# A fused transformer block on one core: expert biases gathered per slot, experts' rows found by a table of token ids, and three first-pass products in seven

## The chip, the cores and the metric

The kernel runs on one core of one Trainium2 chip. The metric is the device time in microseconds (us). The core has a matrix engine (PE in the profile, with its weight loads as PEld), a vector engine (DVE), a scalar engine (ACT), GpSimd (POOL), and SyncE (SP), which here issues the plain transfers; indirect transfers are issued by POOL. Matmul results go to PSUM, operands lie in SBUF, large arrays in DRAM.

## The reference

Two layers work on 8 x 256 = 2048 tokens of 512 channels, all in float32. What the change concerns is the first layer:

```python
xn = layernorm(x)
# attention with decay, 32 heads of 128 channels
q, k, v = silu(xn @ qkv_w.T)
out = gate * normed(attention(q, k, v)) @ out_w.T          # gate = sigmoid(xn @ gate_w.T)
# experts: each token goes to 2 of 16
y = sum over chosen e of ge[e] * (h_e @ w3[e] + b3[e])      # h_e = silu(xn @ w1 + b1) * (xn @ w2 + b2)
z = (silu(xn @ sw1 + sb1) * (xn @ sw2 + sb2)) @ sw3 + sb3   # shared expert
x = x + out + y + z
```

The second layer is a softmax attention with one head of 128 channels and a low-rank mixture of 64 parts; the change touches it in one place, where the last quarter of the residual is fetched.

## The kernel before, in words

**Chunks and the opening (L140 to L525).** The tokens are four chunks of 512 (NCH), each four tiles of 128 rows. In the opening, for each chunk, `normalize` and `turn_rows` give the transposed tokens xT, `token_sums` the sums that the fast products need, `shared_up` and `shared_down` the shared expert, `route` the two chosen experts of each token (`sel_all`) and their gates (`ge`). `shared_down` starts with the experts' last biases: the gates, with a column of ones for the shared bias, are turned by PE (L333), copied by ScalarE (L335) and multiplied by the 17 x 512 matrix of biases (L338) in front of the shared expert's own matmuls (L340). `clear(i)` writes zeros over a DRAM array `xd` of 47 x 128 slots. Behind the chunks, L447 to L523 work out for each token and choice its slot in a list sorted by expert (`slots`), its gate there, and for each tile of 128 slots its expert's weight rows (`rows_`).

**Four passes (L599 to L1215).** Each chunk is one pass i, of 8 groups g of four heads. A group is seven outer products p1 to p7 (a 2 x 2 split of the projection in Strassen's form with seven products instead of eight), in the order of `ORDER`. Each outer product is itself a 2 x 2 product. In passes 1 to 3 its inner products are seven too (`p1()` to `p3()`, L1037 to L1066): some banks are copied by ScalarE (`copied`), joined by DVE and added by POOL (`result`). In the first pass it has eight plain ones (`plain`, L981). The first pass reads the weights from their input array; for the outer products p1, p2 and p4 (`RAW`) they are used as they lie there, for the others DVE first forms outer sums of two or three blocks. POOL then forms four inner sums (`inner_sum`, L634), which are stored in DRAM (`ws`) for the three later passes. An inner product (`product`, L661) is four matmuls of 128 x 128 x 128. Three weight buffers go round (`big`), two staging buffers (`staged`).

**Order.** PE, DVE and SP are ordered by the framework's planner; ScalarE and POOL keep the written order inside the passes (`manual_schedule`, L599), but each engine executes its own list in order. Other work is put between the inner products by `later(after, f)` and `slot()`: every inner product is a slot, and a piece becomes due `after` slots later. So scores, attention, output products, and the experts are interleaved with the projections. `prepare(n + 2)` starts the load of the outer product two ahead; the sums of the next one's weights are made a step per slot (`following.step()`).

**Experts.** In the first pass two tiles of tokens per group are loaded (`row`, L1086) and scattered by POOL to their two slots of `xd` (`scatter`, L1093). From the second pass on, each of 47 tiles of slots is an `Expert` (L689), two or three per group: a plain load of its 128 rows from `xd` (L696), an indirect load of its expert's weights (L697), the turn on PE (L706) 8 slots later, the up product at 11 (L716), the down product at 14 (L728), which ScalarE copies (L733) and SP stores to `yd`. In the last layer the rows are gathered from `yd`, multiplied by the gates and added (`gather`, `settle`).

**End of a pass.** `load_sum` (L933) fetches the stored residual (`xr`, with shared expert and biases), `finish` adds the pass's output. For the last chunk this is done in the last layer (`next_x`, L1289).

## Time and profile before

| | |
|---|---|
| device time, three runs | 2856.99 us median (2852.0 to 2861.1) |
| profiled execution, its own time | 2856.16 us |
| its span, first to last instruction | 2854.4 us |
| mean granted PE clock | 0.993 |
| opening, 0 to 164 us | PE busy 143.8, DVE 96.3, POOL 81.9 us; clock 0.94 |
| first pass, 164 to 765 us | PE busy 588.1, DVE 373.4, POOL 353.3 us; DMA share 0.90 |
| three passes, 765 to 2532 us | PE busy 1752.5 of 1767 us, DVE 909.9, POOL 962.0 us |
| last layer, 2532 us to the end | PE busy 312.2 of 322.4 us |

Busy time is the union of an engine's instructions; matmuls are pipelined, so that a busy PE is occupied but not always at its peak. An "idle before" entry names what released an engine from a wait. DMA share is the mean busy share of the core's 16 DMA engines. Line numbers in the profile are those of the kernel's file; L97 is the helper through which all additions and subtractions go, so those are told apart by their tiles.

### The profile page before, as it was taken

The page shows a single profiled execution, that of the slowest core. Times are in us where ns is not written, and L with a number is a line of the kernel's source. Part 1 is how long each engine was busy: PE and PEld are TensorE (multiplying, and loading weights), DVE is VectorE, ACT ScalarE, POOL GpSimd, SP SyncE. Part 2 cuts the span into 40 slices and gives each one's busy share as a digit, 9 for nine tenths or more (in the row PEclk, how much of TensorE's full clock was granted, in tenths as well). Part 3 has the DMA queues.
Part 4 walks back from the last instruction along what each step waited for, and adds up shares of the span by engine and source line. Part 5 has one row for each costly group of instructions (what it writes and reads, how often), then busy time and mean ns, then how long its engine had stood idle before and what let it go on. Part 6 is the DMA issues. An engine that isn't in the chain of part 4 may idle for free. (4 is left out here: it accounts for less than half of the span.)

```text
span 2854.4 us, 49572 instructions
## 1 busy us (share of the span) xinstructions
PE 2796.7 (98%) x19864; PEld 2566.1 (90%) x19864; DVE 1569.7 (55%) x2615; ACT 948.2 (33%) x1683; POOL 1465.7 (51%) x1213
## 2 busy tenths in 40 slices
PE   8989999999999999999999999999999999999999
PEld 4469999999999999999999999999999999987877
DVE  6555666666654445444545555555555555556663
ACT  3312222212244333333443333443444333432221
POOL 4545666665546555555645454545544566552210
PEclk9999999999999999999999999999999999999999
DMA  7888998899986777778877777777777788652211
GB/s 255 301 309 337 357 352 341 341 349 347 364 320 246 262 266 273 282 270 299 296 265 257 264 266 265 259 274 280 284 259 259 267 310 298 222 212 88 76 61 61
DMA packets 161943, 763.21 MB, mean 267 GB/s; under 512 B 18209, under 2 KB 24225, under 8 KB 109874
## 3 DMA queue, kind: packets, MB, share of 16 engines
q1 hardware_dynamic: 149826, 706.25, 66.9%
q0 software_dynamic: 11888, 53.79, 5.2%
q8 instruction: 157, 2.57, 0.4%
q14 instruction: 72, 0.59, 0.1%
HBM read 596.14 MB, written 163.05 MB: 266 GB/s over the span
## 5 line engine op out<-in xcount | busy, mean ns | idle before, releaser
L666 PE MATMUL ps_a<-xt,w 128*128 128x128 f32 x5376 | 750.9, 276 | 11.7 <-DVE r L97 7.7
L666 PEld LDWEIGHTS ps_a<-xt,w 128*128 128x128 f32 x5376 | 681.9, 192 | 30.1 <-issue 14.3
L97 POOL TENSOR_TENSOR c<-c 128x512 f32<-128x512 f32 x216 | 271.7, 1273 | 262.0 <-DVE c L97 259.9
L97 POOL TENSOR_TENSOR c<-c,r 128x512 f32<-128x512 f32 x240 | 318.4, 1347 | 158.9 <-DVE r L97 153.1
L666 PE MATMUL ps_e<-xt,w 128*128 128x128 f32 x2688 | 373.4, 275 | 1.3 <-DVE c L97 1.3
L97 POOL TENSOR_TENSOR sums<-sums,sq 128x512 f32<-128x512 f32 x120 | 153.3, 1278 | 426.4 <-ACT sq L796 425.6
L996 ACT COPY cp<-ps_a 128x512 f32<-128x512 f32 x336 | 196.4, 585 | 476.0 <-PE ps_a L666 468.8
L666 PEld LDWEIGHTS ps_e<-xt,w 128*128 128x128 f32 x2688 | 344.4, 192 | 11.2 <-issue 3.8
L97 POOL TENSOR_TENSOR w<-w 128x512 f32<-128x512 f32 x224 | 294.6, 1325 | 108.2 <-issue 31.2
L666 PE MATMUL ps_a<-w,xt 128*128 128x128 f32 x1792 | 346.7, 275 | 0.0
L858 PE MATMUL ps_sc<-wo,gT 128*128 128x256 f32 x1288 | 305.1, 379 | 1.8 <-POOL gT L97 1.8
L97 DVE TENSOR_TENSOR acc<-ps_sc,acc 128x512 f32<-128x512 f32 x208 | 143.3, 690 | 265.8 <-PE ps_sc L858 198.8
L666 PEld LDWEIGHTS ps_a<-w,xt 128*128 128x128 f32 x1792 | 272.3, 192 | 0.0
L97 DVE TENSOR_TENSOR c<-ps_a,c 128x512 f32<-128x512 f32 x232 | 157.9, 686 | 202.7 <-PE ps_a L666 201.7
L858 PEld LDWEIGHTS ps_sc<-wo,gT 128*128 128x128 f32 x1288 | 232.3, 190 | 26.8 <-POOL gT L97 2.0
L666 PE MATMUL ps_b<-xt,w 128*128 128x128 f32 x1680 | 236.4, 277 | 6.8 <-ACT c L1010 4.2
L801 DVE SCALAR_TENSOR_TENSOR gT<-ps_o,nw,c 128x256 f32<-128x256 f32 x256 | 112.0, 479 | 231.0 <-ACT sq L796 222.0
L666 PEld LDWEIGHTS ps_b<-xt,w 128*128 128x128 f32 x1680 | 217.3, 194 | 17.5 <-issue 8.2
L744 ACT ACTIVATE c<-c 128x512 f32<-128x512 f32 x256 | 148.9, 627 | 170.1 <-DVE c L97 170.0
L796 ACT ACTIVATE sq<-ps_o 128x512 f32<-128x512 f32 x120 | 71.6, 597 | 382.3 <-PE ps_o L782 382.3
L666 PE MATMUL ps_e<-w,xt 128*128 128x128 f32 x896 | 173.2, 275 | 0.0
L97 DVE TENSOR_TENSOR s<-ps_sc,decay 128x384 f32<-128x384 f32 x256 | 139.8, 552 | 40.7 <-PE ps_sc L770 38.1
(299 smaller groups left out, 4635.8 us busy)
## 6 DMA issues: line engine op xcount, KB each, us to landing
w<-in_w_att_dram SPq DMA_DIRECT2D x128, 1024.0 KB
st<-in_w_att_dram SPq DMA_DIRECT2D x32, 1024.0 KB
wo<-in_w_out_dram SPq DMA_DIRECT2D x113, 256.0 KB
decay<-dec SPq DMA_DIRECT2D x64, 384.0 KB
w<-ws0p SPq DMA_DIRECT2D x12, 1792.0 KB
w<-ws1p SPq DMA_DIRECT2D x12, 1792.0 KB
w<-ws2p SPq DMA_DIRECT2D x12, 1792.0 KB
w<-ws3p SPq DMA_DIRECT2D x12, 1792.0 KB
```

The lines of the kernel that those rows point to most:

```text
L97: (eng or nc.vector).tensor_tensor(o, a, b, op)
L666: mm(bank[:, bass.ts(ty, P)], a, b, start=(first and ty == 0), stop=True, skip_group_check=True,)
L744: nc.scalar.activation(qk, qk, AF.Silu)
L796: nc.scalar.activation(sq, po, AF.Square)
L801: nc.vector.scalar_tensor_tensor(gT[:, h, :].rearrange("p (t n) -> p t n", t=2), po[:, bass.ts(h, S)].rearrange("p (t n) -> p t n", t=2), ...
L858: mm(py[:, bass.ts(t, S)], self.O[p][:, hh, bass.ts(t, P)], self.wo[p][:, hh, :], start=(t == 0 and hh == 0), stop=(hh == 1), skip_group_c ...
L996: nc.scalar.copy(c, bank)
```

## The change

*Last biases.* The gates' column of ones, the turn of the gates, their copy and the bias matmuls leave the opening. Each expert tile gathers its expert's bias row into all 128 partitions (an indirect transfer of POOL, `bias`, by the new list `own_`) into the space that its tokens had, and DVE adds it as it takes the down product out of PSUM, where ScalarE had copied it. The shared expert's bias is added by POOL to the residual where it is fetched (`last_bias`).

*Rows by a table.* `xd`, its clearing, the loads of rows and their scatters go. The 32 scatters stay, five per group, but write only token ids into a DRAM table of one integer per slot. In the first pass's last group the table is read and turned (`read_table`, one PE transpose), and each expert's tokens are gathered from the stored normalized tokens by an indirect transfer of POOL. The turn, bias, up and down stand at 10, 12, 13 and 18 slots.

*Sevenfold.* In the first pass, the outer products p1, p2 and p4 are made of seven inner ones as in the later passes, with the tokens' sums formed once by POOL (`first_sums`). Their inner weight sums come in a new order, that of 7 first, and those that are left when the outer product starts are made ahead of it. The next weights are prepared behind the last product of the outer product before.

*Space.* `before`, `sel_all` and the gates move from the opening's pool to the space of the accumulator; `dist` moves into the opening's pool. The store of the residual keeps its written place.

```diff
-    def once(shape, name):
-        return work.tile(shape, FP, tag=name, name=name, bufs=1)
+    def once(shape, name, dtype=FP):
+        return work.tile(shape, dtype, tag=name, name=name, bufs=1)
+    disp = Parts(accp.tile([P, 7 * CH], FP, tag="acc", name="disp"))
...
-    b3_t = held[0 : E + 1, SH * C : (SH + 1) * C]
-    nc.sync.dma_start(out=b3_t, in_=b3)
...
-    xd = dram.tile([NSLOT, C], FP, name="xd")
+    table = dram.tile([NSLOT, 1], I32, name="table")
...
-    xnd = [dram.tile([P, TPC, C], FP, name=f"xnd{i}") for i in range(NCH)]
+    xnd = dram.tile([NT, C], FP, name="xnd")
...
-    zero = held[:, (SH + 1) * C : (SH + 2) * C].unsqueeze(1)
-    nc.gpsimd.memset(zero, 0.0)
+    none = once([NMT, P], "none", I32)
+    nc.gpsimd.memset(none, 0)
+    nc.sync.dma_start(out=table.rearrange("(j p) o -> j (p o)", p=P), in_=none)
...
-        tt(ge[:, :, 0:E], sc, sel, ALU.mult)
-        nc.vector.memset(ge[:, :, E : E + 1], 1.0)
+        tt(ge, sc, sel, ALU.mult)
...
         xc = xs[i]
-        pg = ps_sc()
-        for t in range(TPC):
-            nc.tensor.transpose(pg[0 : E + 1, bass.ts(t, P)], gates[i][:, t, :], ident)
-        gT = work.tile([E + 1, CH], FP, tag="geT", name="geT", bufs=1)
-        nc.scalar.copy(gT, pg[0 : E + 1, :])
...
-            mm(py, gT[:, bass.ts(t, P)], b3_t, start=True, stop=False)
...
-                mm(py, hT[:, e, bass.ts(t, P)], w3sh[:, e, :], start=False, stop=(e == SH - 1))
+                mm(py, hT[:, e, bass.ts(t, P)], w3sh[:, e, :], start=(e == 0), stop=(e == SH - 1))
...
-    sel_all = once([P, NTT, E], "sel_all")
+    sel_all = disp.tile([P, NTT, E], FP, name="sel_all")
...
-        nc.sync.dma_start(out=xr[i], in_=xs[i])
+        tc.keep_in_program_order(nc.sync.dma_start(out=xr[i], in_=xs[i]))
...
             if i == 0:
+                t = first_x[p]
...
-                    nc.sync.dma_start(out=blocks(first_x[p][:, 0:4]), in_=y)
+                    nc.sync.dma_start(out=blocks(t[:, 0:4]), in_=y)
+                if p in RAW:
+                    first_sums.append(t)
...
-    def clear(i):
-        lo, hi = (0, 12, 24, 36, NMT)[i : i + 2]
-        nc.sync.dma_start(
-            out=xd[lo * P : hi * P, :].rearrange("(j p) c -> p j c", p=P),
-            in_=zero.to_broadcast([P, hi - lo, C]),
-        )
...
-        nc.sync.dma_start(out=xnd[i], in_=xns[i])
+        nc.sync.dma_start(
+            out=xnd[i * CH : (i + 1) * CH, :].rearrange("(t p) c -> p t c", p=P), in_=xns[i]
+        )
...
-        ge = once([P, TPC, E + 1], f"ge{i}")
+        ge = disp.tile([P, TPC, E], FP, name=f"ge{i}")
...
-        clear(i)
...
-    disp = Parts(accp.tile([P, 7 * CH], FP, tag="acc", name="disp"))
+    own_ = const.tile([P, NMT], I32, name="own_")
+    whose = const.tile([P, NMT], I32, name="whose")
+    token = const.tile([P, NTT], I32, name="token")
+    nc.gpsimd.iota(token, pattern=[[P, NTT]], base=0, channel_multiplier=1)
...
+    def last_bias(r, t3):
+        nc.sync.dma_start(out=t3, in_=b3[E : E + 1].to_broadcast([P, C]))
+        for t in range(TPC):
+            add(r[:, t, :], r[:, t, :], t3, nc.gpsimd)
...
                     f(w[:, o], w[:, a_], w[:, b_], pool)
-                    if o == 7:
+                    if o == 6:
...
-                    partial(inner_sum, *at) for at in ((add, 4, 0, 3), (sub, 5, 4, 1), (sub, 6, 2, 5), (sub, 7, 1, 0))
+                    partial(inner_sum, *at) for at in ((sub, 7, 1, 0), (add, 4, 0, 3), (sub, 5, 4, 1), (sub, 6, 2, 5))
...
+                if p in RAW:
+                    return sums_of(w)
...
+            return sums_of(w)
+        def sums_of(w):
...
+            if i == 0 and p in RAW:
+                x_ = first_x[p]
+                return dict(zip(("p1", "p7", "p2", "p3", "p5", "p6", "p4"), (x_[:, n] for n in range(7))))
...
                 )
+        for t in first_sums:
+            sub(t[:, 4], t[:, 1], t[:, 0], nc.gpsimd)
+            sub(t[:, 1], t[:, 3], t[:, 1], nc.gpsimd)
+            sub(t[:, 5], t[:, 3], t[:, 4], nc.gpsimd)
+            sub(t[:, 6], t[:, 2], t[:, 5], nc.gpsimd)
...
-                n += getattr(f, "func", f).__name__ not in ("silu", "gate", "row", "scatter", "load_sum", "sums1", "sums2", "sums3", "sums4", "settle0", "settle1", "out_sum")
+                n += getattr(f, "func", f).__name__ not in ("silu", "bias", "gate", "read_table", "scatter", "load_sum", "sums1", "sums2", "sums3", "sums4", "settle0", "settle1", "out_sum")
...
                 self.xe, self.we = xw[:, 0:C], xw[:, C:]
-                nc.sync.dma_start(out=self.xe, in_=xd[bass.ts(j, P), :])
+                nc.gpsimd.indirect_dma_start(
+                    out=self.xe, out_offset=None, in_=xnd[:, :],
+                    in_offset=bass.IndirectOffsetOnAxis(ap=whose[:, j : j + 1], axis=0),
+                    bounds_check=NT - 1, oob_is_err=False,
+                )
...
+
+            def bias(self):
+                nc.gpsimd.indirect_dma_start(
+                    out=self.xe, out_offset=None, in_=b3[:, :],
+                    in_offset=bass.IndirectOffsetOnAxis(ap=own_[:, self.j : self.j + 1], axis=0),
+                    bounds_check=E, oob_is_err=False,
+                )
...
                 ye = attn.tile([P, C], FP, tag="sum", name="ye", bufs=3)
-                nc.scalar.copy(ye, py)
+                add(ye, py, self.xe)
...
                     nc.sync.dma_start(out=self.r, in_=xr[self.i])
+                    last_bias(self.r, attn.tile([P, C], FP, tag="sum", name="sb3", bufs=3))
...
                 slot()
+                if self.following:
+                    self.following.step()
...
             e = Expert(j)
-            later(8, e.turn)
-            later(11, e.up)
-            later(14, e.down)
-        def row(t):
-            x_ = attn.tile([P, C], FP, tag="sum", name="row", bufs=3)
-            nc.sync.dma_start(out=x_, in_=xnd[t // TPC][:, t % TPC, :])
-            for n in range(TOP):
-                later(6 + 10 * n, partial(scatter, x_, t, n))
-        def scatter(x_, t, n):
+            later(10, e.turn)
+            later(12, e.bias)
+            later(13, e.up)
+            later(18, e.down)
+        def scatter(t, n):
...
-                out=xd[:, :],
+                out=table[:, :],
...
-                in_=x_, in_offset=None, bounds_check=NSLOT - 1, oob_is_err=False,
+                in_=token[:, t : t + 1], in_offset=None, bounds_check=NSLOT - 1, oob_is_err=False,
...
+        def read_table():
+            rows = attn.tile([P, P], I32, tag="h1", name="rows")
+            nc.sync.dma_start(out=rows[0:NMT], in_=table.rearrange("(j p) o -> j (p o)", p=P))
+            byno = attn.tile([P, P], FP, tag="he", name="byno")
+            def turn_table():
+                nc.vector.tensor_copy(byno[0:NMT], rows[0:NMT])
+                pt = ps_sc()
+                nc.tensor.transpose(pt[:, 0:NMT], byno[0:NMT, :], ident[0:NMT, 0:NMT])
+                nc.vector.tensor_copy(whose, pt[:, 0:NMT])
+            later(16, turn_table)
...
+
+        def sevenfold(n):
+            return plan[n][0] > 0 or plan[n][2] in RAW
...
-                    for e in range(2):
-                        later(1 + 24 * e, partial(row, 2 * g + e))
+                    for e in range(5 * g, min(5 * g + 5, TOP * NTT)):
+                        later(5 + 10 * (e - 5 * g), partial(scatter, e // TOP, e % TOP))
+                    if g == NG - 1:
+                        later(4, read_table)
...
             u.load_out(k)
-            if i == 0:
+            last = outers[n - 1] if n and sevenfold(n - 1) else None
+            if not sevenfold(n):
+                if last:
+                    last.p3()
                 prepare(n + 2)
                 cur.plain(outers[n + 1])
                 continue
+            if i == 0:
+                while cur.steps:
+                    cur.step()
+                cur.following = outers[n + 1]
             cur.p1()
             cur.p7()
-            if plan[n - 1][0] > 0:
-                outers[n - 1].p3()
+            if last:
+                last.p3()
             prepare(n + 2)
             cur.p6()
             cur.p4()

...
             nc.sync.dma_start(out=x_, in_=xr[i])
+            last_bias(x_, work.tile([P, C], FP, tag="sb3", name="sb3", bufs=1))
```

More of the change, by code (lines that the diff above doesn't have):

```diff
@@ L199, in block_kernel @@
     nc.gpsimd.memset(ones, 1.0)
-    before = once([P, E, E], "before")
+    before = disp.tile([P, E, E], FP, name="before")
     nc.gpsimd.memset(before, 1.0)
@@ L206, in block_kernel @@
     )
-    dist = const.tile([P, S + P], FP, name="dist")
+    dist = once([P, S + P], "dist")
     nc.gpsimd.iota(
@@ L365, in block_kernel @@
     HC = NC // 2
-    first_x, first_w = {}, []
+    first_x, first_w, first_sums = {}, [], []
     def token_sums(i):
@@ L501, in block_kernel @@
     nc.vector.tensor_reduce(own, owner, AX.X, ALU.add)
+    nc.vector.tensor_scalar(own_, own, float(E - 1), None, ALU.min)
     nc.vector.tensor_scalar(own, own, float(E - 1), float(P), ALU.min, ALU.mult)
@@ L521, in block_kernel @@
             at_i = bass.ts(i, TPC)
-            tt(hit[:, at_i, :], hit[:, at_i, :], gates[i][:, :, 0:E], ALU.mult)
+            tt(hit[:, at_i, :], hit[:, at_i, :], gates[i], ALU.mult)
         nc.vector.tensor_reduce(slot_gates[:, n, :], hit, AX.X, ALU.add)
@@ L965, in __init__ @@
                 self.steps = []
+                self.following = None
                 self.w = weights(unit.i, unit.g, p, self.steps)
```

## The prediction

> **What bounds the kernel now.** I read first the page's busy times and its row of granted clock, then the same by stretches, then TensorE's own timeline, its waits, and last the other engines where the change adds work. Of the page:
>
> ```profile
> PE 2796.7 (98%) x19864; PEld 2566.1 (90%) x19864; DVE 1569.7 (55%) x2615; ACT 948.2 (33%) x1683; POOL 1465.7 (51%) x1213
> PEclk9999999999999999999999999999999999999999
> ```
>
> Busy alone would prove little, since matmuls overlap. Two of the stretches (us; busy us of PE, PEld, DVE, ACT and POOL with counts; clock; DMA share; GB/s), one of the first pass and one of the second:
>
> ```profile
> 390.00:465.00 75.00, 75.00 (x585) 72.53 (x584) 46.10 (x73) 16.29 (x28) 45.80 (x37) 1.00 0.90 345
> 841.00:917.00 76.00, 76.00 (x581) 72.09 (x581) 33.31 (x53) 32.62 (x61) 40.58 (x33) 1.00 0.70 256
> ```
>
> To see that PE is full and not only occupied, I add up a group of heads. The chain of waits gives the real rates, start to start:
>
> ```profile
> 2139.91 1.78 PE ps_a L666 x16
> 2141.70 1.73 PE ps_sc L858 x8
> ```
>
> A float32 matmul leaves two records, so an inner product (four 128x128 matmuls) is 8 records, 0.893 us, and four 128x256 matmuls cost 1.73 us. A group of the first pass has 56 inner products (50.0), 32 plain output matmuls of 128x256 (13.8), and for attention 16 pairs of a 256- and a 128-column matmul (16 x 0.657 = 10.5): 74.3 us. The saved sums of groups 1 and 7 start at 241.2 and 684.3 in the trace, 73.9 us apart per group. PE is the bound, nearly to the last us, and one inner product less is worth 0.893 us while nothing else becomes late.
>
> The opening is PE's too, but looser. PE's timeline there (start, duration, operation, idle before it):
>
> ```profile
> 141.85 1.98 PE L340 MATMUL ps_a<-held,scratch 128*128 128x512 f32 x4
> 147.41 0.61 PE L333 MATMUL ps_sc<-ident,ge 128*17 128x128 f32 x4 [3.58 <-DVE ge L97]
> 147.86 0.60 PE L482 MATMUL ps_sc<-sel_all,disp 128*128 128x256 f32 x2
> ...
> 149.58 2.07 PE L338 MATMUL ps_b<-held,geT 17*128 17x512 f32 x2
> 151.58 3.78 PE L340 MATMUL ps_b<-held,scratch 128*128 128x512 f32 x4
> ...
> 158.41 1.12 PE L338 MATMUL ps_e<-held,geT 17*128 17x512 f32 x2
> 159.46 1.98 PE L340 MATMUL ps_e<-held,scratch 128*128 128x512 f32 x4
> ```
>
> L338 is a bias matmul, L340 the shared experts' two, L333 the transposes of the gates, and the one real gap is PE waiting for them. The first pass starts at 164.4. The experts' gathers, in the answer on the weights' rows:
>
> ```profile
> L697 POOL DMA_INDIRECT xw<-in_w_exp_dram,rows__1106 x47: 1005/1011/1053, 764.0 to 2211.2; - x47
> DMA to landing us min/median/max: 6.9/7.5/13.0
> ```
>
> **The Trainium skill.** "TensorE: Matmul & The Clock Gate", Part 1, says that the array falls to half its clock after an idle window of about 3.4 us. The trace agrees: behind the 3.58 us gap the same L340 group takes 3.78 us instead of 1.98. "DMA: Bandwidth & Descriptors", SWDGE vs HWDGE vs iDMA, says that indirect transfers come from GpSimd, whose cores compute the descriptors. The trace agrees (all 47 gathers stand on POOL) and prices one: 1.01 us of POOL, about 7.5 us to landing. "SBUF — State Buffer", Who interferes with whom, says that a VectorE instruction with two SBUF inputs contends with a GpSimd one that reads SBUF; the 32 VectorE weight sums w<-w run 674 to 2156 ns here, so more POOL work may also stretch VectorE.
>
> **The change, part by part** (sums against the span of 2854.4; the profiled execution took 2856.16, 1.8 more, 0.8 below the median of 2856.99).
>
> *1. Opening, expert biases off PE.* Gone are 16 matmuls with the 17-row gate tile, 16 transposes and 4 ScalarE copies. In the first three chunks a bias matmul takes 1.05 us start to start (158.41 to 159.46 is such a pair), 12 x 1.05 = 12.6; in the last 2.00, 1.20, 1.05, 1.05 = 5.3. The transposes with their wait for the copy take 1.26 us each time (three times: 3.8), the last with the wait for the gates 4.0 (143.83 to 147.86), and the half clock behind that gap costs 1.8 on L340. Sum 27.5. Not all will come: VectorE's routing chain of the last chunk (16 us, scores at 130.8 to selection at 146.8) does not shrink, and the small counting matmuls that need it stand somewhere in PE's queue. If they stand ahead of the shared experts' last matmuls, PE waits up to 8.5 us: the chain starts about 11 us earlier (two chunks' biases) and ends near 136, PE reaches them near 127.5. Also gone are four clears of 12 MB in all (about 9 us of transfer each at 340 GB/s), behind which POOL waits 10 to 16 us per chunk for stores of sums; that gives slack, not time. The 12 sums on x (0.45 us each, 5.4) fit POOL's idle 18.5 to 39 us. I take -24; bounds -16 and -28.
>
> *2. The seam into the first pass.* Before, PE lost 4.2, 1.7 and 2.2 us at 171 to 199, the first since ScalarE's first copy waited for the counting's last reads of tiles under it. Those tiles (selection, gates, "before") move to the accumulator's space. But the residual's store, issued behind PE's last opening matmul, still holds space below the new tiles for about 4 us, and now the very second product needs a ScalarE copy. I take 0, bounds -5 and +5.
>
> *3. First pass, three outer products in seven.* 24 inner products less: 24 x 0.893 = -21.4. Per group it adds 6 ScalarE copies (6 x 0.585 = 3.5), 3 VectorE adds (2.1) and 6 POOL adds (1.31, mean of the two c rows, 7.9), and POOL issues five scatters instead of four where there are any left. POOL per group: 28 inner sums x 1.325 = 37.1, sums of squares 5.1, scatters 4.2 make 46.4, as the stretch shows (45.8); after it 55 of 71.6 us, 77%. VectorE 49 of 71.6. So neither is a new bound by volume. What changes is the due time: the POOL sums of p1, p2 and p4 were only for storing, now the outer product itself reads them. In group 4 the stores behind these sums go out at 463.4, 472.9 and 530.3, and the outer products start at 463.3, 476.5 and 527.9. For p4 the last sum is 2.4 us late, but the new order makes first what the second product reads, and the last is read by the fifth or later. Tight, and just enough. Preparing comes two or three products later in these outer products, so loads lose about 3 us of lead; before, SyncE mostly waited there for stores anyway. I charge +2 in all, bounds 0 and +20.
>
> *4. Dispatch.* 16 row loads and 32 scatters of 256 KB become 32 scatters of 128 ids: 12 MB of some 200 less in the pass, DMA share 0.9, no gain on PE. The table's turn is one PE transpose.
>
> *5. Experts, 47 times.* POOL gets two more indirect transfers (2 x 1.01, 95 us over 1770, from about 43 to 49 of 76); the tokens' plain load leaves SyncE; the result's move goes from ScalarE (0.585) to VectorE (0.69). POOL works in written order, so its lag counts. From the weights' gather to PE's first turn it is now 12.7 us for a group's first expert, 9.2 for its second, 6.6 for its third (872.44, 894.57, 920.38): POOL is up to 6 us behind. The turn comes two slots later (some 3 us): 9.6 us for a landing of about 7.5 and a little more POOL work. The bias gather waits for the turn; behind it stand POOL's adds into c and, through them, ScalarE's silu. It has 6 slots, some 9 us, until VectorE adds it: 8.5 plus POOL's lag. In the second pass a few of these will be late by 1 or 2 us, which holds VectorE and sometimes PE. In later passes POOL's lag is small (12.7 and 11.3 us). I take +4, bounds 0 and +20.
>
> *6. Last bias.* Three times 4 POOL adds (5.2 us) at a pass's end, and once in the last layer, where the residual lands at 2728.3, VectorE's finish runs to 2731.1 and the next use is at 2736.8: hidden; uncovered it would cost 5. I charge +2 in all.
>
> Sum: -24 + 0 - 21.4 + 2 + 4 + 2 = -37.4, span 2817, time **2819 us** (-1.3%).
>
> **Rivals.** (B) POOL paces the first pass: with 77% and waits in order, the sums of the three outer products come late. Against it: the order of the sums and 16 us per group of slack; for it: p4's margin. At 0.6 us per such product (24) it takes 14: 2833. (D) The opening stays bound by the routing chain and the residual's store: only -16 and a worse seam, +5: 2832. B and D together, 2846. (C) Slower: a late bias or token gather stops VectorE, then PE, at each expert. From 1.0 us of PE per expert (47 on top of the forecast) it is slower by over 0.3%; a landing of 13 us, the longest seen, is 5.5 above the median; if a quarter of that reached PE, it would be 1.4 us each, 66 in place of my 4: 2881. It is one mechanism, the gathers' landing against the 6 slots of the bias. Against it: in the trace PE never waits for a gather, and the deadlines were moved with the work. (N) Stalls at the gathers of 0.8 us per expert just balance the gain: within 0.3%, about 2856. That the change would not do what it says is excluded for the products, since the diff leaves out their matmuls.
>
> **How the numbers follow.** My forecast 0.60, B or D or both 0.26, N 0.05, C 0.09. Below 0.3% (8.6 us) a measurement of this kernel can't tell a change. So faster 0.86, same 0.05, slower 0.09. The likeliest case has 2808 to 2829. With every gain in full and no cost (-28 - 5 - 21.4) it would be 2802; the low end, 2805, lies between. The high end, 2847, is B with D (2846). Below the low end I leave some 5 in 100, above the high end N and C, 14.
>
> **What would show it.** Group starts in the first pass 71.6 us apart and PE full there; no L333 or L338 work; the first product near 140 instead of 164; POOL 75 to 78% in the first pass. Wrong, if PE's waits there name POOL's weight sums or DVE adds fed by them (B), if the first product starts past 150 (D), or if PE or VectorE waits on the experts' gathers (C).

## The result: 4.3% slower, and where the profile shows it

The changed kernel took 2976.76 us (median of four runs, 2973.13 to 2988.74) against 2856.9: a ratio of 1.043, 95% interval 1.039 to 1.046. The forecast was 2819. Its profiled execution took 2979.63 us with a span of 2977.9, 123.5 more than the span before.

The page of the changed kernel, with the two lines that answer to those shown of before, and the transfer rate in 40 slices of 74.4 us:

```profile
PE 2799.4 (94%) x19625; PEld 2573.8 (86%) x19625; DVE 1647.6 (55%) x2685; ACT 945.8 (32%) x1679; POOL 1651.1 (55%) x1384
...
PEclk8889999898999999999999999999999999999999
GB/s 258 262 254 245 259 256 235 242 261 253 322 351 311 278 271 273 269 271 269 301 309 264 266 266 266 269 269 309 285 267 266 280 297 299 235 185 133 73 59 59
```

PE has 239 matmul records fewer and yet isn't busy for less time; its share falls from 98 to 94%. The clock's digit falls to 8 only within the first ten slices, and in the same slices the rate stays near 250 GB/s (235 to 262), where the kernel before had up to 357. From the eleventh slice on, 322 and 351, the two kernels look alike.

By stage, from PE's own timeline. The stages are parted by the first product of the first pass, then by the matmul over the sums of squares with which a pass's finish begins (some 35 us into the next pass, so that each stretch has its seam in it), then by the end:

| stretch, us | before | after | difference |
|---|---|---|---|
| opening, to the first product | 164.4 | 141.8 | -22.6 |
| first pass with its seam | 633.8 | 758.2 | +124.4 |
| second pass | 607.8 | 618.9 | +11.1 |
| third | 587.8 | 592.5 | +4.7 |
| fourth | 557.8 | 559.1 | +1.3 |
| last layer | 302.8 | 307.4 | +4.6 |

The two stretches that answer to those of before are one group of the first pass and 76 us of the second (same columns: length, busy us of PE, PEld, DVE, ACT and POOL with counts; clock; DMA share; GB/s):

```profile
413.90:510.50 96.60, 77.64 (x555) 73.03 (x554) 51.53 (x75) 19.45 (x35) 55.42 (x45) 0.91 0.96 251
944.00:1020.00 76.00, 74.71 (x568) 70.70 (x567) 36.26 (x55) 29.66 (x55) 48.21 (x40) 1.00 0.77 281
```

A group takes 96.6 us instead of 73.9. PE stands still for 19 of them, and the mean clock is 0.91. The DMA engines count as busier than before (0.96 against 0.90) while they move 251 GB/s instead of 345: each packet takes longer. PE's waits in the first pass, in us, times, longest:

```profile
PE ps_a L675 <- DMA w<-in_w_att_dram: 30.4, 6, 9.0
PE ps_sc L906 <- DVE gT L829: 29.2, 9, 9.2
PE ps_sc L906 <- DVE s L97: 26.9, 5, 8.1
```

The first is a wait for weights by name. The other two come by way of DVE, whose queue stood for 61.9 us from 200 to 800 us at weight blocks that hadn't landed (21.4 us before):

```profile
DVE w L97 <- DMA w<-in_w_att_dram: 39.7, 6, 11.7
DVE w L97 <- DMA st<-in_w_att_dram: 22.2, 6, 8.2
```

POOL's weight sums, the sign of rival B, come to 1.4 us here. Rival C's sign, waits for the experts' gathers, would stand in the later passes: PE has none there, and VectorE waits for the bias gather five times, 8.2 us in all.

What happens around one of the 32 scatters? POOL issues one at 334.73. Some stretches of 2 us behind it (a packet is counted whole in the stretch in which it starts, so that a DMA share can be above 1):

```profile
338.00:340.00 2.00, 1.96 (x16) 1.72 (x14) 0.00 (x0) 0.00 (x0) 0.25 (x1) 1.00 1.00 418
340.00:342.00 2.00, 0.00 (x0) 0.00 (x0) 0.00 (x0) 0.00 (x0) 0.00 (x0) 1.00 2.23 229
342.00:344.00 2.00, 0.05 (x1) 0.05 (x1) 1.86 (x4) 0.00 (x0) 0.00 (x0) 1.00 0.79 119
344.00:346.00 2.00, 2.00 (x5) 1.64 (x6) 1.18 (x3) 0.00 (x0) 0.00 (x0) 0.52 0.62 82
346.00:348.00 2.00, 2.00 (x9) 1.64 (x9) 2.00 (x4) 0.00 (x0) 0.00 (x0) 0.63 0.62 217
348.00:350.00 2.00, 1.18 (x9) 0.93 (x7) 2.00 (x5) 0.00 (x0) 0.00 (x0) 1.00 0.99 377
```

Some 5 us behind the issue the rate falls from 418 to 229, 119 and 82 GB/s and needs about 8 us to recover. PE has nothing to do for 4 us and then runs at about half its clock (0.52), as the Trainium skill says of the idle window ("TensorE: Matmul & The Clock Gate", Part 1). The next scatter, issued at 356.48, is followed by the same dip (22 GB/s from 364 to 366 us), there without a stop of PE. Added up against 418 GB/s, the last five stretches moved some 2.1 MB less (1066 GB/s short in sum, by 2 us): by this estimate that much is held up by 128 ids, 512 bytes in all. The scatters themselves, with issue to landing:

```profile
L1121 POOL DMA_INDIRECT table<-token,slots x32: 992/993/1297, 153.0 to 740.7; - x32
...
DMA to landing us min/median/max: 10.8/11.9/15.2
```

They land in 11.9 us; the scatters of 2 KB rows before took 7.3 (each from the four of 32 whose landing the trace has). The last stands at 740.7, and behind it the rate recovers.

PE's real rates, where it isn't waiting, are those of before (the chain of waits in a later pass: start us, us):

```profile
2266.94 1.73 PE ps_sc L886 x8
...
2269.56 1.79 PE ps_a L675 x16
```

The opening went as forecast. PE there (answering to the lines of L333, L338 and L340 before):

```profile
138.35 1.88 PE L334 MATMUL ps_e<-held,scratch 128*128 128x512 f32 x4
140.07 1.88 PE L334 MATMUL ps_a<-held,scratch 128*128 128x512 f32 x4
141.78 0.83 PE L675 MATMUL ps_a<-xt,w 128*128 128x128 f32 x6
```

The shared expert's matmuls follow one another without a transpose or a bias matmul, and the first product stands at 141.8. The three gathers of an expert (tokens, weights, bias), each with its DMA time:

```profile
L712 POOL DMA_INDIRECT xw<-xnd,whose x47: 998/1017/1058, 864.2 to 2330.8; - x47
DMA to landing us min/median/max: 4.0/5.1/8.4
...
L717 POOL DMA_INDIRECT xw<-in_w_exp_dram,rows__1047 x47: 992/996/1004, 865.5 to 2332.1; - x47
DMA to landing us min/median/max: 7.5/8.9/11.1
...
L732 POOL DMA_INDIRECT xw<-in_b_dram,own__1048 x47: 1013/1019/1292, 892.8 to 2350.2; - x47
DMA to landing us min/median/max: 4.4/5.7/7.4
```

### The profile page after: what moved, and what is told of

It reads as the page before. It is cut to its first block, busy times and chain, and to the rows that moved or that the text cites. A ratio compares the mean times of both kernels' runs of the same rounds, so it can differ in the third digit from the quotient of the medians.

```text
span 2977.9 us, 49421 instructions
## 1 busy us (share of the span) xinstructions
PE 2799.4 (94%) x19625; PEld 2573.8 (86%) x19625; DVE 1647.6 (55%) x2685; ACT 945.8 (32%) x1679; POOL 1651.1 (55%) x1384
## 4 chain that ended last, share of the span: by engine, by line
PE 70%; DMA 13%; DVE 8%; issue 5%; POOL 3%; ACT 0%; SPq 0%; DVEq 0%; POOLq 0%; ACTq 0%
PE ps_a L675 20%; PE ps_e L675 10%; PE ps_sc L886 9%; PE ps_b L675 5%; DMA w<-in_w_att_dram 3%; PE ps_o L809 3%; PE ps_sc L744 3%; PE ps_sc L797 3%; DMA st<-in_w_att_dram 2%; POOL w L97 2%; PE ps_a L1567 2%; DVE w L97 2%; PE ps_sc L906 2%; PE ps_o L810 2%; PE ps_sc L798 1%
## 5 line engine op out<-in xcount | busy, mean ns | idle before, releaser
L675 PE MATMUL ps_a<-xt,w 128*128 128x128 f32 x5376 | 761.1, 278 | 48.0 <-DMA w<-in_w_att_dram 30.4
L675 PEld LDWEIGHTS ps_a<-xt,w 128*128 128x128 f32 x5376 | 695.5, 194 | 75.2 <-issue 44.4
L97 POOL TENSOR_TENSOR c<-c 128x512 f32<-128x512 f32 x240 | 303.0, 1278 | 292.3 <-DVE c L97 276.5
L97 POOL TENSOR_TENSOR c<-c,r 128x512 f32<-128x512 f32 x264 | 347.8, 1338 | 174.3 <-DVE r L97 172.4
L1028 ACT COPY cp<-ps_a 128x512 f32<-128x512 f32 x384 | 223.9, 584 | 633.3 <-PE ps_a L675 603.2
L886 PE MATMUL ps_sc<-wo,gT 128*128 128x256 f32 x1288 | 304.8, 379 | 1.8 <-POOL gT L97 1.8
L675 PE MATMUL ps_b<-xt,w 128*128 128x128 f32 x1536 | 218.8, 279 | 15.0 <-DVE w L97 4.8
L97 DVE TENSOR_TENSOR c<-ps_a,c 128x512 f32<-128x512 f32 x216 | 146.8, 686 | 149.5 <-PE ps_a L675 144.8
L675 PEld LDWEIGHTS ps_b<-xt,w 128*128 128x128 f32 x1536 | 199.0, 195 | 23.3 <-issue 17.5
L906 PE MATMUL ps_sc<-wo,gT 128*128 128x256 f32 x576 | 151.8, 411 | 56.0 <-DVE gT L829 29.2
```

Source lines behind the costliest of these rows:

```text
L97: (eng or nc.vector).tensor_tensor(o, a, b, op)
L675: mm(bank[:, bass.ts(ty, P)], a, b, start=(first and ty == 0), stop=True, skip_group_check=True,)
L886: mm(py[:, bass.ts(t, S)], self.O[p][:, hh, bass.ts(t, P)], self.wo[p][:, hh, :], start=(t == 0 and hh == 0), stop=(hh == 1), skip_group_c ...
L906: mm(py[:, bass.ts(h, S)], gT[:, hh, bass.ts(t, P)], self.wo[pair, h][:, hh, :], start=(h == 0 and hh == 0), stop=(hh == 1), skip_group_ch ...
L1028: nc.scalar.copy(c, bank)
```

## Experiments

The theory from these readings, H1: each scatter of 128 four-byte ids into a table without gaps stalls the other transfers. Rivals: H2, the sevenfold products are fed late; H3, the moved arrays in DRAM make all traffic slower. "Group" below is the mean time from group 1 to group 7 of the first pass, by each group's first store of weight sums: 73.85 us before, 93.4 after (five scatters per group, two in the last of these). The stores wander against PE by about a microsecond per group, which is nothing beside 20 us; where less is at stake, PE's own order is used below. The diffs are against the changed kernel unless another is named.

### Is it the scatters?

*no_scatter*, the scatters left out and nothing else:

```diff
-                    for e in range(5 * g, min(5 * g + 5, TOP * NTT)):
-                        later(5 + 10 * (e - 5 * g), partial(scatter, e // TOP, e % TOP))
```

> The changed kernel without its 32 scatters of token ids; the table keeps the spread numbers it is filled with at the start, so the experts work on other tokens, with the same number of instructions. Theory H1 (each scatter of 128 four-byte ids holds up the other transfers for about 8 us, and the first pass lives on them): the first pass, from the first product to its sum-of-squares matmul, falls from 758 us to about 612 (634 before, less 21 for the sevenfold products), and the whole to about 2830 us. Rival H2 (the sevenfold products of the first pass are fed too late by GpSimd's sums and by loads with a shorter lead): the first pass stays above 735, the whole above 2950. Rival H3 (other addresses in DRAM make all traffic of the pass slower): as H2, and the rate between 300 and 600 us stays near 250 GB/s, where H1 expects over 330.

2842.41 us, 0.993 of before (0.991 to 0.996). The first pass falls by 132 us to 626.2, with 325 GB/s between 300 and 600 us. H1 holds; H2 and H3 fall as causes of the loss. But 626 isn't 612: the sevenfold products don't bring their 21 us here. (The expectation speaks of spread numbers in the table. As run, the table kept its zeros, so that every gather fetched token 0. The three later passes took 617.8, 592.9 and 559.1 us, those of plain_no_scatter below, which has spread numbers, 617.6, 594.2 and 557.9: the fill hardly matters.)

*table_alone*, the kernel before with the table, its scatters and the token gathers, and with the moved tiles and the experts' later slots that they need (against the kernel before):

```diff
-                nc.sync.dma_start(out=self.xe, in_=xd[bass.ts(j, P), :])
+                nc.gpsimd.indirect_dma_start(
+                    out=self.xe, out_offset=None, in_=xnd[:, :],
...
-                out=xd[:, :],
+                out=table[:, :],
...
-                in_=x_, in_offset=None, bounds_check=NSLOT - 1, oob_is_err=False,
+                in_=token[:, t : t + 1], in_offset=None, bounds_check=NSLOT - 1, oob_is_err=False,
```

> The kernel before with the table dispatch alone (ids side by side as in the change, token gathers, no clears), without the gathered biases and without the sevenfold products. If the scatters alone make the loss, the first pass goes from 634 to about 750 to 760 us and the whole to about 2965 to 2980. If they hurt only together with the sevenfold products, which leave less slack to loads and sums: first pass 680 or less, the whole under 2905.

3008.08 us, 1.051 (1.048 to 1.054); a group takes 94.8 us. The scatters make the loss without the sevenfold products: 21 us per group, between 4 and 5 us each. The whole is even above the expectation. Some 16 us of that stand in the opening (first product at 180.3 instead of 164.4), ahead of the first scatter at 191.8, so they aren't the scatters': from 119 to 180 us the mean clock is 0.72 there, before it was 0.92 from 119 to 164. Why isn't traced.

### What in the scatter?

*ids512* scatters rows of 128 copies of the id:

```diff
-    table = dram.tile([NSLOT, 1], I32, name="table")
+    table = dram.tile([NSLOT, 128], I32, name="table")
...
+            nc.gpsimd.iota(ids[:, 0:128], pattern=[[0, 128]], base=t * P, channel_multiplier=1)
...
-                in_=token[:, t : t + 1], in_offset=None, bounds_check=NSLOT - 1, oob_is_err=False,
+                in_=ids[:, 0:128], in_offset=None, bounds_check=NSLOT - 1, oob_is_err=False,
```

*ids4_pitch512* scatters the same four bytes, but to slots 512 bytes apart:

```diff
-    table = dram.tile([NSLOT, 1], I32, name="table")
+    table = dram.tile([NSLOT * 128, 1], I32, name="table")
...
+    nc.vector.tensor_scalar(ends_, ends_, 128.0, None, ALU.mult)
+    nc.vector.tensor_copy(wide, ends_)
...
-                out_offset=bass.IndirectOffsetOnAxis(ap=slots[:, n, t : t + 1], axis=0),
+                out_offset=bass.IndirectOffsetOnAxis(ap=wide[:, n, t : t + 1], axis=0),
```

> The changed kernel with each id scattered as a row of 128 copies (512 bytes at a pitch of 512), one small GpSimd fill per scatter more. If the stall comes from elements of 4 bytes: gone, first pass about 615 us, the whole near 2835. If any indirect scatter that comes five to a group does it: unchanged, 2970. If the closeness of the targets does it, they are 128 times further apart here, so it would be gone too; the run with four bytes at that pitch tells the two apart.

> The changed kernel with each id still four bytes, but the slots 512 bytes apart in DRAM. If the closeness of the targets makes the stall (all 128 ids of a scatter into 24 KB): gone, near 2835 us. If it is the four-byte element: unchanged, first pass about 755, the whole near 2975. H2 and H3: unchanged as well.

2882.08 (1.007, 1.004 to 1.010) and 2883.05 us (1.008, 1.005 to 1.011), so they agree. At this distance the size of the element doesn't matter; the distance does. Most of what is left above 2842 is one wait of PE, by way of DVE, for the table's read, which has become 6016 pieces of four bytes (PE's waits from 640 to 780 us, four bytes at a pitch of 512):

```profile
PE ps_b L679 <- DVE c L97: 27.1, 1, 27.1
```

and DVE's in the same stretch:

```profile
DVE byno L1138 <- DMA rows<-table: 29.6, 1, 29.6
```

DVE stands 29.6 us at the table's ids with the products' sums queued behind. That a strided last dimension becomes one descriptor per element is in the Trainium skill ("DMA: Bandwidth & Descriptors", Rules for kernel authors); here it costs 27 us once, even with the table's turn due eight slots later in these runs.

*ids_turned* keeps the table at 24 KB and turns its order, so that neighbouring slots are 188 bytes apart and each partition reads its own 47 ids in one piece:

```diff
+    nc.vector.tensor_scalar(high, slots, 7, None, ALU.arith_shift_right)
+    nc.vector.tensor_scalar(wide, slots, P - 1, None, ALU.bitwise_and)
+    nc.vector.tensor_scalar(wide, wide, float(NMT), None, ALU.mult)
+    tt(wide, wide, high, ALU.add)
...
-            nc.sync.dma_start(out=rows[0:NMT], in_=table.rearrange("(j p) o -> j (p o)", p=P))
+            nc.sync.dma_start(out=whose, in_=table.rearrange("(p j) o -> p (j o)", p=P))
```

> The changed kernel with the table of the same 24 KB in another order: slot s stands at (s mod 128) x 47 + s / 128, so neighbouring slots are 188 bytes apart, and each partition reads its 47 ids in one piece, with no turn on TensorE and none of the 6016 four-byte reads that the run with a pitch of 512 bytes paid for with one wait of 27 us. If the stall comes from several ids of one scatter falling into the same few tens of bytes: gone, first pass about 626 us as without scatters, the whole near 2842. If it comes from all 128 falling into one region of 24 KB: unchanged, first pass about 755, the whole near 2975.

2842.89 us, 0.994 (0.992 to 0.996): as fast as without scatters, and faster than before. The scatters have the same instruction, the same bytes and the same 24 KB; only the order of their targets differs. The changed kernel between 300 and 600 us:

```profile
300.00:600.00 300.00, 237.53 (x1678) 224.00 (x1677) 156.97 (x229) 59.25 (x104) 169.60 (x132) 0.90 0.95 249
```

and with the turned table, and its scatters' landing:

```profile
300.00:600.00 300.00, 294.43 (x2241) 281.69 (x2240) 214.88 (x310) 78.22 (x139) 225.04 (x172) 1.00 0.87 324
...
DMA to landing us min/median/max: 2.2/5.4/8.9
```

PE is busy for 294 of 300 us instead of 238, and a scatter lands in 5.4 us instead of 11.9.

### How close is too close?

The same edit as for the pitch of 512 bytes, at 64, 32, 16 and 8, with the factor 16, 8, 4 and 2:

```diff
-    table = dram.tile([NSLOT, 1], I32, name="table")
+    table = dram.tile([NSLOT * 16, 1], I32, name="table")
```

> As the run with four-byte ids at a pitch of 512 bytes, but at 64 bytes (the table is 385 KB), with the same strided read of 6016 ids at the end. If ids that share 64 bytes make the stall: as at 512, the whole near 2883. If ids up to somewhere below 188 bytes apart still disturb each other: between 2890 and 2970.

> Four-byte ids at a pitch of 32 bytes, so that two neighbouring slots share 64 bytes; else as the runs at 64 and 512. If what may not be shared is 32 bytes or less: as at 64 and 512, first pass near 655 and the whole near 2882. If it is 64 bytes: part of the stall is back, landing above the 6.0 us of pitch 64, and the whole between 2895 and 2950.

> Four-byte ids at a pitch of 16 bytes, so that two neighbouring slots share 32 bytes. If 32 bytes are what may not be shared: a part of the stall is back, landing above the 6.1 us of pitch 32 and the whole above 2885. If it is 16 bytes or less: as at 32, near 2878.

> Four-byte ids at a pitch of 8 bytes. At 16 bytes there was no stall (landing 6.3 us, DMA 327 GB/s between 300 and 600 us), at 4 bytes a full one (11.9 us, 249 GB/s). If a stall grows with the number of ids that fall into the same few tens of bytes: part of it is here, landing 7 to 10 us, the whole 2895 to 2940. If only ids that follow one another without a gap stall: none, near 2880.

| pitch, bytes | landing, median us | GB/s, 300 to 600 us | first pass, us | time, us |
|---|---|---|---|---|
| 4 (the change) | 11.9 | 249 | 758 | 2976.8 |
| 8 | 8.8 | 301 | 690 | 2920.0 |
| 16 | 6.3 | 327 | 655 | 2887.7 |
| 32 | 6.1 | 327 | 657 | 2877.1 |
| 64 | 6.0 | 327 | 656 | 2880.8 |
| 512 | 5.7 | 327 | 652 | 2883.1 |
| 188 (turned, read in one piece) | 5.4 | 324 | 625 | 2842.9 |

From 8 to 512 the first pass has the read's wait of some 27 us in it. The last column holds more than the scatters: at 8 bytes the opening is 12 us longer as well (first product at 153.8 instead of 141.8), so the first pass is the better measure. The landing times at 4 and 8 bytes are from four scatters of 32, the others from 28 or more.

The effect is gradual: full at 4, partly there at 8, not seen from 32 on. The run at 16 bytes doesn't decide. Its rate and first pass are those of 32 and above, but both marks that had been set for a shared 32 bytes were just reached: landing 6.3 us (above 6.1) and the whole 2887.7 (above 2885), and the DMA share between 300 and 600 us is 0.91, where 32 and 64 bytes have 0.89 at the same rate (first 16, then 32 bytes):

```profile
300.00:600.00 300.00, 295.79 (x2261) 283.80 (x2260) 211.48 (x305) 80.32 (x142) 226.07 (x176) 1.00 0.91 327
300.00:600.00 300.00, 295.87 (x2260) 283.91 (x2260) 213.71 (x310) 80.76 (x143) 224.43 (x173) 1.00 0.89 327
```

Its profiled execution is the fastest of its four, 8.6 us under the median. So a small remnant at 16 is possible. For the buffers of collectives, the Trainium skill asks for an alignment of 32 bytes, to prevent a read-modify-write by the hardware ("Collectives: The Full Stack", Rules for kernel authors). The runs say that writes of four bytes are not slow by themselves, since they are fine at 32 and above; whether several writes into the same 32 bytes queue behind one another, and at how many it begins to tell, no run shows.

### What are the sevenfold products worth?

*seven_alone* is the kernel before with the change's sevenfold part only; *seven_late* delays its row scatters as well:

```diff
+            if i == 0 and p in RAW:
+                x_ = first_x[p]
+                return dict(zip(("p1", "p7", "p2", "p3", "p5", "p6", "p4"), (x_[:, n] for n in range(7))))
...
-                later(6 + 10 * n, partial(scatter, x_, t, n))
+                later(14 + 6 * n, partial(scatter, x_, t, n))
```

> The kernel before with the sevenfold products of the first pass alone. The predicted step was 24 inner products of 0.893 us less and 2 us of cost: 2838 us. The rival that GpSimd's and VectorE's sums come late (0.6 us per outer product, 14 in all) gives 2850; the changed kernel without its scatters had a first pass only 8 us shorter than before, which speaks for the rival.

> The kernel before with the sevenfold products alone, and the row scatters due at 14 and 20 slots behind their row load instead of 6 and 16. Alone, the sevenfold products made it 23 us slower, and once per group GpSimd stood about 7 us at a row scatter that waited for its row, with the inner weight sums behind it. If that waiting is the cause: TensorE's waits for sums in the groups shrink, and the whole comes to 2845 to 2860. If GpSimd's and the transfers' volume is the cause (12 MB of rows beside 71% busy GpSimd): unchanged, 2875 to 2885.

2880.47 us (1.008, 1.005 to 1.010) and 2939.26 us (1.028, 1.026 to 1.030). Slower alone, and still slower with the scatters late: my reason, GpSimd standing at its rows, was wrong. DVE's waits in the two runs name what I had overlooked, first seven_alone:

```profile
DVE r L97 <- DMA xd<-row,slots: 22.6, 5, 6.0
```

then seven_late:

```profile
DVE r L97 <- DMA xd<-row,slots: 47.2, 6, 9.9
```

The copied row and the product's joined result `r` take the same three buffers, and `r` must wait until a row's scatter has landed. (The first pass is 55 us longer in seven_late than in seven_alone, so these waits aren't all of it.) In the change this can't happen, since it has no rows; so seven_alone wasn't the change's part alone. *seven_own* gives the rows a buffer of their own:

```diff
-            x_ = attn.tile([P, C], FP, tag="sum", name="row", bufs=3)
+            x_ = attn.tile([P, C], FP, tag="sq", name="row", bufs=1)
```

> The kernel before with the sevenfold products alone, and the copied rows in a buffer of their own instead of the three that the sevenfold form's joined results (r) use as well. When the rows shared them, VectorE waited for the row scatters to land, 22.6 us in five waits, and 47.2 us when the scatters came later. If this sharing is the whole cost: the predicted 2838 us, at most 2845. If GpSimd's work in order and the rows' transfers take the rest, as the pair with the gathered biases says (2864 with, 2860 without the sevenfold form): 2852 to 2862.

2860.21 us, 1.001 (1.000 to 1.002): 20 us back, but no gain from 24 products less. By the marks set for it (2852 to 2862), the shared buffer was only part of the cost. Four more runs complete the pairs. *rows_copied* is the change with the old dispatch (rows in their own buffer):

```diff
-                out=table[:, :],
+                out=xd[:, :],
...
-                in_=token[:, t : t + 1], in_offset=None, bounds_check=NSLOT - 1, oob_is_err=False,
+                in_=x_, in_offset=None, bounds_check=NSLOT - 1, oob_is_err=False,
```

*bias_alone* is that without the sevenfold form, *turned_noseven* the turned table without it, and *plain_no_scatter* leaves out the scatters of turned_noseven, as no_scatter does, and fills the table with spread numbers. The core of what undoes the sevenfold form:

```diff
-            return plan[n][0] > 0 or plan[n][2] in RAW
...
-            if i == 0:
-                while cur.steps:
-                    cur.step()
-                cur.following = outers[n + 1]
```

> The changed kernel with the old dispatch: expert rows cleared, loaded, scattered in 2 KB rows and read back plainly; the gathered biases and the sevenfold products stay. H1: the first pass is at about 612 to 620 us, and the passes behind it lose less than the 17 us that the changed kernel loses, since one gather per expert is gone: 2815 to 2830 us, under both kernels. H2: first pass above 735, the whole 2940 to 2960.

> The kernel before with the gathered last biases and the moved tiles alone: no table, no sevenfold products. The opening's step was -24 us, the experts' +4 and the last bias +2: 2839 us. By the runs so far the three later passes and the last layer give back some 15 us, and the residual's store, behind the clears' transfers, holds the first ScalarE copy for up to 24 us at the seam (here the first product doesn't need that copy, so less): 2850 to 2870 us.

> The kernel with the turned table, with the sevenfold products of the first pass undone (eight plain ones again). If the sevenfold form is worth what its 24 inner products weigh, less the predicted 2 us: first pass about 644 us and the whole about 2862, against 624.9 and 2842.9. If waits for sums eat most of it: first pass about 632 to 636, the whole near 2850. If it costs on balance, as it did added alone to the kernel before (+23 us): the whole under 2843.

> The kernel with the turned table and eight plain products in the first pass, without its 32 scatters; the table keeps the spread numbers that it is filled with, so the experts work on other tokens. With the spread scatters a group of this kernel took 77.3 us, 3.5 more than the 73.85 of the kernel before. If scattered ids still cost transfers something even when they stand 188 bytes apart: a group falls to about 73.9 us, the whole to about 2832 to 2840. If it is something else in the pass (SyncE's order, the freed row loads): the group stays near 77, the whole near 2858.

Here a group is taken from PE's own order: a sixth of the time from group 1 to group 7 by the first product of scores with values (281.69 to 731.91 us in the kernel before; the trace has all of these matmuls in every run).

| beside | plain: group, time in us | sevenfold: group, time in us |
|---|---|---|
| row copies, biases on PE | 75.0, 2856.9 | 74.2, 2860.2 (seven_own) |
| row copies, gathered biases | 74.6, 2860.5 (bias_alone) | 74.1, 2864.2 (rows_copied) |
| turned table | 78.5, 2859.6 (turned_noseven) | 74.2, 2842.9 (ids_turned) |
| no scatters | 75.0, 2845.1 (plain_no_scatter) | 74.0, 2842.4 (no_scatter) |

A group ought to have come down by 2.7 us. In three pairs it comes down by 0.5 to 1.0, and the whole gains 2.7 us at most; beside row copies the whole even loses 3 to 4. Only beside the turned table do both gain more, and there the plain partner is the slow one. (Two traces of the same first pass, ids_turned and turned_slots below, differ by 1.3 us per group, 74.2 and 72.9, so that the whole times say more than a single trace. The two kernels without scatters differ in the table's order and fill too.) So PE's work isn't the only thing that holds a group near 74 us. From 250 to 700 us, PE's busy time before and in seven_own:

```profile
sum 450.00, PE 447.53 PEld 431.73 DVE 280.25 ACT 97.88 POOL 275.86; mean PE 149.18 PEld 143.91 DVE 93.42 ACT 32.63 POOL 91.95
sum 450.00, PE 439.92 PEld 421.31 DVE 303.02 ACT 120.35 POOL 328.60; mean PE 146.64 PEld 140.44 DVE 101.01 ACT 40.12 POOL 109.53
```

In six groups 16 us of products went, and 7.6 us of that came back as idle time. PE's waits in seven_own from 130 to 830 us, apart from the seam, are many and small: 4.4 us for DVE's scores, 3.9 for POOL's weight sums, 3.4 for DVE's. Which of DMA, POOL and DVE stands behind them, the runs don't single out. The scatters at 188 bytes aren't free in every company either: beside plain products they cost 3.5 us per group (78.5 against 75.0) and 14.5 us of the whole, beside sevenfold ones nothing that shows. The runs rows_copied (2815 to 2830 expected) and plain_no_scatter (2832 to 2840, or 2858) missed their marks.

bias_alone and rows_copied also price the clears. In both the first product comes at 133, earlier than in the change, and then PE stands (PE's timeline in bias_alone: start, duration, operation, idle before it):

```profile
163.78 1.65 PE L668 MATMUL ps_b<-xt,w 128*128 128x128 f32 x6 [21.88 <-ACT c L1021]
```

and ScalarE's, whose copy it waits for:

```profile
163.15 0.58 ACT L1021 COPY c<-ps_b 128x512 f32<-128x512 f32 x1 [41.70 <-DMA xr<-x]
```

The copy's space is freed by the residual's last store, which SyncE issues at 157.7 us here and at 143.9 in the change. With the table there are no clears, and this wait was 4.1 us (7.5 in ids_turned); up to that point rows_copied (24.5 us) differs from the change in nothing but the dispatch, of which the clears are the largest part. By which way they delay the store isn't traced: SyncE's list has stores of token sums in front of it, for which it waits on POOL.

### The experts' 17 us

After, in the second pass, PE's largest wait is

```profile
PE ps_sc L744 <- DVE xeT L728: 7.9, 7, 1.3
```

that is, the up product waits for DVE to take the turned tokens out of PSUM; a DVE addition into `c` stands in front. bias_alone, which has no token gather, shows the same (7.7 us in six waits), so it's the new slots and not the gather. *turned_slots* moves one thing in ids_turned:

```diff
-            later(10, e.turn)
+            later(9, e.turn)
```

> The kernel with the turned table, with the experts' turn at 9 slots instead of 10, so that VectorE takes the turned tokens out of PSUM one slot earlier before the up product. If the second pass's 9 us are TensorE's waits for that copy (7.9 us in seven waits): second pass 609 to 611 us instead of 617, the whole about 2836. If the token gather then comes too late (7.2 us to landing, longest 12.3): waits for it appear, the whole 2843 or more.

2832.04 us, 0.990 of before (0.988 to 0.993), the fastest version. The second pass falls from 617.1 to 609.8 (607.8 before). The first pass is 6.5 us shorter too (618.4 against 624.9), and it is shorter in groups in which the edit changes nothing (72.9 us against 74.2), so only some 7 of the 12 us between the two profiled executions are the edit's. PE's waits in the second pass are down to

```profile
PE ps_a L681 <- DVE r L97: 2.4, 3, 1.6
PE ps_sc L732 <- DMA xw<-xnd,whose: 1.1, 1, 1.1
```

The 7.9 us are gone; one token gather comes 1.1 us late. DVE's waits for the bias gathers stay (10.7 us in six, 8.2 in five in the change).

## Why the prediction was wrong

**The step that failed is 4, Dispatch,** "no gain on PE", charged at nothing. It counted bytes: 256 KB per scatter less. It priced POOL's issue (right, 0.99 us) and left out what a transfer does to the transfers beside it. The cost was 132 us by no_scatter, some 4 us per scatter, and it's set by how near the targets stand. It hit this stage because the first pass lives on its loads; the view that I quoted for "PE is full" had the DMA share at 0.90 beside it. I used that only to say that fewer bytes don't help, not that slower transfers would hurt at once. None of the rivals had it; C, the slower one, was about gathers at the experts: PE's waits after name none of those, and VectorE's come to 8.2 us, far from the loss. The range had no room for it.

**1, Opening:** right, -22.6 for -24. But "that gives slack, not time", said of the clears, was wrong by bias_alone: with clears kept, the seam gives 22 us back.

**2, Seam:** right in place and size: 4.1 us for the ScalarE copy, then 2.6 and 4.8, 11.5 in all against 8.1 before, within the 5 of the bound. But that holds only without the clears, as bias_alone shows.

**3, Sevenfold:** wrong as a gain. The 24 products are gone, but only one pair of runs gives anything like -19 (-16.7, with a plain partner that its scatters slow down); without scatters the time falls by 2.7 us, beside rows it rises by 3.3 and 3.7. The step took PE's time per product as the group's time. Rival B had the better size: at 0.6 us per product it leaves 0.9 of the 2.7 us per group, and three pairs show 0.5 to 1.0. Its reason is shown in part only: in seven_own PE's waits for POOL's and DVE's weight sums are 3.9 and 3.4 us in the whole stretch.

**5, Experts:** the term was too small, 17.1 us in three passes against +4, within its bounds of 0 and 20. Not for the landing or POOL's lag that I worked through, but for the copy out of PSUM between turn and up: 7.9 of the second pass's 11.1 us, gone with one slot. The rest (2 us in the second pass and some 9 us in passes three and four of turned_slots, by its spans of 593.8 and 561.1) I haven't traced. Landing times came near the estimated 7.5: 5.1 us for the tokens, 8.9 for the weights, 5.7 for the bias.

**6, Last bias:** +2 forecast for all passes together; the last layer alone is 4.6 us longer (3.7 in bias_alone, 1.3 in rows_copied). The uncovered 5 that I had set aside was nearer, though the runs don't isolate it.

Put together for the turned table: -22.5 in the opening, -8.9 in the first pass, +18.3 in the later ones, +3.7 in the last layer, -9.4 in the span, and with the experts' turn a slot earlier -21.6 (of this last step 6.5 us stand in the first pass, which the edit doesn't change).

## What to carry to other kernels

Where a stage lives on transfers, ask of every new small transfer what it does to those beside it, not only how many bytes it has; here a DMA share of 0.90 was the warning. Ids or flags that are scattered to DRAM should not stand side by side: an order in which neighbours are 32 bytes or more apart costs a few index operations, and one that suits the reader saves its strided read too. Before undoing one part alone, look which buffers it shares with a part that the change took away.

## What the hardware did that I hadn't expected

128 four-byte writes from one indirect transfer, into a DRAM table without gaps, held the core's transfers below 418 GB/s for some 8 us, at the lowest 82; at 32 bytes or more between the targets nothing of it was seen beside the sevenfold products (beside plain ones, scatters at 188 bytes still cost 14.5 us in all), at 16 at most a remnant, at 8 bytes about a quarter of the loss (first pass 690 us against 655 at 16, the read's 27 us in both, where the change without that read had 758). The size of the element made no difference: 512-byte rows and four-byte ids at the same pitch of 512 gave 2882 and 2883 us.
